# Phase two of a graph and expert kernel: gathers asked for at another distance, two flows on their own spans, degrees counted one phase sooner

## The chip, the cores and the metric

The kernel runs on one core of one Trainium2 chip. The metric is the device time of one execution in microseconds; the time before is 3418.66 us, the median of three runs (3414.97 to 3419.67). The engines named below are PE (matrix products), DVE (vector work), ACT (activations and copies), POOL (which here issues nearly only gathers and scatters) and SP (which issues the plain DMAs). Each works through its own list of instructions in order.

## The reference, cut to what matters

There are 3125 nodes with 256 features, 50000 edges sorted by destination, and four blocks, each a graph step and a feed-forward step. The change lies in the first two graph steps, which share one pass over the edges, and in the preparation of the third:

```python
# block 0: messages by relation type, summed by destination, then experts
transformed = jnp.einsum('ni,rio->rno', h, weight)
msg = transformed[rel_type, src] * norm
out = jax.ops.segment_sum(msg, dst, num_segments=h.shape[0])
...
out = out + combine[:, e:e + 1] * y      # 8 experts, the top 2 of them weighted
# block 1: messages by species and edge features
msgs = embed_table[node_z][senders] * W
agg = jax.ops.segment_sum(msgs, receivers, num_segments=node_feats.shape[0])
out = jnp.concatenate([node_feats, agg], axis=1) @ W_comb + b_comb
# block 2 and 3 need the edges of each node: attention and a maximum
m = jax.ops.segment_max(e, edge_dst, num_segments=N)
```

## The kernel before

**Edges.** The 50000 edges are padded to 392 windows of 128, in 49 groups of 8. The rows of two windows of a group are gathered by one call of `fetch_rows` (L810), which issues two indirect DMAs on POOL (L153, tile `g`); we call that a row pair. A group has four pairs. Twelve pairs have buffers (`G_PAIRS`), so pair n can only be gathered when the group of pair n - 12 has been summed. `make_hots` (L821) makes the group's 0/1 mask on DVE, and `add_up` (L829) multiplies mask and rows on PE (L834), copies the result out of PSUM on ACT (L837) and has SP store it to a table of partial sums in DRAM (L839, L842): 288 rows for each group, `part1` in phase one and `part0` in phase two.

**Phase one** (100 to 649 us) takes the pairs of block 1, from the table of species, and beside them PE makes the table of block 0 (`chunk`, L618). One background step `next(bg)` runs at every second pair; the background is `ranks` (L1180), which finds where each node's edges begin, its degree, and in which rows of the partial sums they lie. It ends at 288 us and the rest of the phase has none.

**Phase two** (`stage_two`, L908) takes the pairs of block 0 in 392 slots, eight for each group: slot 8g + j. The first twelve pairs have been asked for at the end of phase one. In every odd slot from slot 9 on one more pair is asked for; the mask of the next group is made in slot j = 1, the group is summed in slot j = 7, and `between` (L1143) then advances everything else by a slot. At slot 16 stands `all_edges` (L722), a branch that is not taken with sorted edges.

**Flows.** Node tiles of 128 are worked on in 13 flows, flow 0 of one tile and the others of two. A flow is born when all its edges have been summed (slots 32, 64, 96, ...; 32 apart). It has its partial sums gathered (`load_p`, tile `p`, one gather for each tile, waiting for the stores that it reads) 6 slots later (`LOAD_AFTER`), starts 14 slots after its birth (`START_AFTER`), and runs through three parts, each a generator that is spread evenly over a span of slots: `route` (L960, 22 steps over 24 slots: adds the sums, norm, top 2), `experts` (L1005, 32 steps over 30) and `combine` (L1033, 34 steps over 30, with the sums of phase one, and the tables of block 2). One part is never worked on by two flows. After slot 392 the flows that are left run without a clock.

**Background of phase two.** At every second slot one step runs of `by_degree` (L1273) and then `records` (L1352). `by_degree` orders the nodes by degree: it counts the nodes of each degree (L1282 compares, L1288 adds, one product with ones and a scan: `base`), then for each of 25 tiles it ranks the nodes (L1305 adds `base`, L1306 the nodes of earlier tiles, L1307 those ahead in this tile, all three into one PSUM bank; L1309 picks the rank), and then turns ranks into order (`both`, L1325: a compare at L1328 and three at L1330 for each tile, and a product at L1340). `records` then makes edge scores from 100 loads of attributes, stores them (L1384), and fetches for each of 25 tiles the window of its nodes' edges (`k_w`, a gather on POOL).

The order of instructions on each engine is that of the program: no scheduler moves them.

Of the kernel before, what the change touches and what calls it, by code (L numbers as in the profile page):

```python
# [9 lines left out]
F32 = mybir.dt.float32  # L10
# [9 lines left out]
P = 128  # L20
N = 3125
NT = 25
# [37 lines left out]
G_PAIRS, F_BUFS = 12, 4  # L60
# [14 lines left out]
LAST = [8 * g - 9 if g < NG else NW - 2 for g in DONE]  # L75
SEGS = [g - 1 if g < NG else NG for g in DONE]
assert all(2 * P * (t + k) <= n * SEG for (t, k), n in zip(FLOWS, SEGS))
LOAD_AFTER, START_AFTER = 6, 14
AB = 4


# [27 lines left out]
BG_EVERY = 2  # L109
# [3 lines left out]
def tile_gnn_ffn(ctx: ExitStack, tc: tile.TileContext, a: dict, out: bass.AP):  # L113
    nc = tc.nc
# [52 lines left out]
    ones = per.tile([P, P], F32, name="ones")  # L167
# [216 lines left out]
    wb = w1st.enter_context(tc.tile_pool(name="wb", bufs=1))  # L384
# [72 lines left out]
    with tc.If(uns > 0):  # L457

        rec = dram.tile([E, RW], F32, name="rec")
        with tc.tile_pool(name="srt", bufs=1) as ep, tc.tile_pool(name="srt2", bufs=2) as eb, \  # L460
# [12 lines left out]
            beg = before_nodes(ep, eb, hif, lof, "s_")  # L473
# [10 lines left out]
            for b in range(ET // BT):  # L484
# [11 lines left out]
                for i in range(BT):  # L496
                    j = b * BT + i
# [173 lines left out]
    def late_weights(pool, w):  # L671

        def loads(name, dst, src):
            w[name] = dst
            nc.sync.dma_start(dst, src)

        def rows(m, name):
            k, n = m.shape
            return pool.tile([P, k // P, n], F32, name="w_" + name, bufs=1), m.rearrange("(k p) n -> p k n", p=P)

        def same(src, n):
            return bass.AP(tensor=src.tensor, offset=src.offset, ap=[[0, P], [1, n]])

        loads("rw0", *rows(a["L0_ffn_router_w"], "rw0"))
        loads("b01", pool.tile([P, 16], F32, name="w_b01", bufs=1), a["L0_ffn_b1"])
        loads("b02", pool.tile([8, D], F32, name="w_b02", bufs=1), a["L0_ffn_b2"])
        yield
        w["01"], w["02"] = (wbig[:, i * 16 * D : (i + 1) * 16 * D].rearrange("p (e k f) -> p e k f", e=8, k=2) for i in range(2))
        for e in range(8):
            nc.sync.dma_start(w["01"][:, e], a["L0_ffn_w1"][e].rearrange("(k p) f -> p k f", p=P))  # L690
            nc.sync.dma_start(w["02"][:, e], a["L0_ffn_w2"][e].rearrange("(f p) d -> p f d", p=P))
            yield
        loads("c", *rows(a["L1_gnn_W_comb"], "c"))
        yield
        nc.sync.dma_start(wfa[:, :, :D], a["L2_gnn_W_func"].rearrange("(k p) n -> p k n", p=P))
        loads("bc", pool.tile([P, D], F32, name="w_bc", bufs=1), same(a["L1_gnn_b_comb"], D))
        for i in range(2):
            loads(f"aw{i}", pool.tile([P, D], F32, name=f"w_aw{i}", bufs=1), same(a["L2_gnn_W_att"][:, i * D : (i + 1) * D], D))
        loads("wr", pool.tile([P, D], F32, name="w_wr", bufs=1), same(a["L1_ffn_wr"], D))
        yield  # L700
# [76 lines left out]
    def stage_one():  # L777
# [24 lines left out]

        sh = w1st.enter_context(tc.tile_pool(name="sh", bufs=2))
        w = {}
        bg, loads = ranks(sh), late_weights(sh, w)
        pairs = NW // 2
        rows, feats, hots = {}, {}, {}
        at = {"rows": 0, "feats": 0, "chunk": LEAD}
# [35 lines left out]
        with tc.tile_pool(name="ea", bufs=1) as ea, psums(t=2, pw=3, agg=1, w=2):  # L844
# [35 lines left out]
            for k in range(pairs):  # L880
                g = k // 4
# [26 lines left out]
    def stage_two(eb, bg, w, rows, hots, fetch_rows, make_hots, add_up):  # L908
# [199 lines left out]

        class Flow:

            PARTS = ((route, 22, 24), (experts, 32, 30), (combine, 34, 30))

            def __init__(self, q):
                self.q, self.part, self.gen, self.born, self.loaded = q, 0, None, slot, False
# [1 line left out]
            def step(self, slot, older, fast):  # L1116
                if self.part == 3:
                    return
                make, total, span = self.PARTS[self.part]
                if not self.loaded and slot >= self.born + LOAD_AFTER:  # L1120
                    self.loaded = True
                    load_p(self.q, 0)
                if slot < self.born + START_AFTER:
                    return
                if self.gen is None:
                    if any(o.part <= self.part for o in older):
                        return
                    self.gen, self.since, self.done = make(self.q), slot, 0
                due = self.done + 1 if fast else -(-total * (slot - self.since + 1) // span)
                while self.done < due:  # L1130
                    self.done += 1
                    try:
                        next(self.gen)
                    except StopIteration:
                        assert abs(self.done - 1 - total) < 3 or size(self.q) == 1, (self.part, self.done - 1)
                        self.part, self.gen = self.part + 1, None
                        return
# [3 lines left out]
        slot = 0  # L1141

        def between(fast=False):  # L1143
            nonlocal slot
            for i, f in enumerate(flows):
                f.step(slot, flows[:i], fast)
            while flows and flows[0].part == 3:
                flows.pop(0)
            if slot % BG_EVERY == 0:
                next(bg, None)  # L1150
            if slot >= 60 and slot % 2:
                next(zeros_, None)
            slot += 1

        made = 0
        make_hots(0, nrmW)
        for g in range(NG):
            if g == 2:
                all_edges(bank())
            for j in range(8):  # L1160
                if j == 1:
                    make_hots(g + 1, nrmW)
                if j % 2 and g:
                    fetch_rows()
                if j == 7:
                    add_up(g, [rows.pop(pairs + 4 * g + i) for i in range(4)], part0)
                between()
            while made < len(DONE) and DONE[made] == g + 1:
                flows.append(Flow(made))
                made += 1  # L1170
# [99 lines left out]

    kept = {}

    def by_degree(sh):  # L1273

        node, deg, beg = kept["node"], kept["deg"], kept["beg"]
        key = wb.tile([P, NT], F32, name="k_key")
        nc.vector.tensor_scalar(key, deg, 127.0, -1.0, op0=OP.min, op1=OP.mult)
        nc.vector.tensor_scalar_add(key, key, 127.0)
# [1 line left out]
        def chosen(t):  # L1280
            s = sh.tile([P, P], F32, name="k_sel")
            nc.vector.tensor_scalar(s, iota_f, key[:, t : t + 1], None, op0=OP.is_equal)  # L1282
            return s
# [2 lines left out]
        nc.vector.memset(cum, 0.0)  # L1286
        for t in range(NT):
            nc.vector.tensor_add(cum, cum, chosen(t))  # L1288
            if t % 4 == 3:
                yield  # L1290
        pk = tp(P)
        nc.tensor.matmul(pk, ones, cum, start=True, stop=True)
        tot = wb.tile([P, P], F32, name="k_tot")
        base = wb.tile([P, P], F32, name="k_base")
        nc.vector.tensor_copy(tot, pk)
        nc.vector.tensor_tensor_scan(base, ones, tot, 0.0, op0=OP.mult, op1=OP.add)
        nc.vector.tensor_sub(base, base, tot)
        rank = wb.tile([P, NT], F32, name="k_rank")
        prev = wb.tile([P, P], F32, name="k_prev")
        nc.vector.memset(prev, 0.0)  # L1300
        nxt = chosen(0)
        for t in range(NT):
            sel, nxt = nxt, (chosen(t + 1) if t + 1 < NT else None)
            pk = tp(P)
            nc.tensor.matmul(pk, ones[:1, :], base[:1, :], start=True, stop=False)  # L1305
            nc.tensor.matmul(pk, ones, prev, start=False, stop=False)  # L1306
            nc.tensor.matmul(pk, upper, sel, start=False, stop=True)  # L1307
            nc.vector.tensor_add(prev, prev, sel)
            stt(sel, sel, 1.0, pk, op0=OP.mult, op1=OP.mult, accum_out=rank[:, t : t + 1])  # L1309
            yield  # L1310
# [1228 lines left out]
```

## Time and profile before

| What | Value |
| --- | --- |
| median of three runs | 3418.66 us (3414.97 to 3419.67) |
| profiled execution, its own time | 3418.41 us |
| its span | 3416.7 us |
| phase one from its first products of edges | 100 to 649 us |
| phase two, 392 slots | 649 to 1315 us |
| flows left after the last slot | 1315 to 1470 us |
| PE, DVE, POOL busy in phase two's slots (666 us) | 528.36, 471.49, 441.43 us |

A stretch row gives, for a stretch of the span, the busy time of each engine with its number of instructions, the granted TensorE clock as a share of full speed, and the DMA's share and rate. A row of the order of time gives start, length, engine, line, operation and tiles; what stands in brackets is how long the engine had been idle before it and what ended that. A gather's bar on POOL (0.95 us) is followed by 0.30 us in which the queue issues nothing else.

### The profile page before, as it was taken

Reading aid. Unit: us, or ns where it says so; the run is one execution under the profiler, and the core shown is the slowest. Engines: PE = TensorE matmul, PEld = TensorE weight load, DVE = VectorE, ACT = ScalarE, POOL = GpSimd, SP = SyncE. Lnnn points to the kernel's source line nnn. Section 1 sums busy time; section 2 is a strip of 40 time slices with the busy share of each in tenths; the row PEclk is TensorE's granted clock in tenths of the full one; section 3 lists DMA queues with packets and bytes.
Section 4 is the critical chain, followed back from the end, with each engine's and each line's share of the span. In section 5 each row is a group of like instructions: output and inputs, shape, how many; then the busy total and the mean of one; then the engine's idle time right before and its main releaser. Section 6 shows DMA issues by size and latency. Waiting matters only on the chain. (4 is left out here: it accounts for less than half of the span.)

```text
span 3416.7 us, 36379 instructions
## 1 busy us (share of the span) xinstructions
PE 2240.7 (66%) x10325; PEld 1557.2 (46%) x10325; DVE 1678.1 (49%) x6067; ACT 898.8 (26%) x2016; POOL 1999.7 (59%) x2265
## 2 busy tenths in 40 slices
PE   4689999777888779849322585877711212259993
PEld 1334444345666557637211373756511112237672
DVE  2343333557787766533365565566723333366211
ACT  1334545312233223312110131323300000024341
POOL 3677777766666671011577777764467777732433
PEclk9889999758999889959655696888755555559997
DMA  7577777857775452031243585876233333325562
GB/s 238 183 229 245 254 253 251 255 135 228 235 235 177 111 144 80 31 130 50 80 111 104 158 262 176 266 257 188 95 90 106 105 105 106 105 76 165 166 217 81
DMA packets 246803, 553.65 MB, mean 162 GB/s; under 512 B 49584, under 2 KB 131251, under 8 KB 240174
## 3 DMA queue, kind: packets, MB, share of 16 engines
q0 software_dynamic: 103296, 283.74, 27.8%
q1 hardware_dynamic: 137624, 261.43, 23.6%
q10 hardware_dynamic: 5654, 5.88, 0.6%
q8 instruction: 90, 1.47, 0.2%
q14 instruction: 139, 1.14, 0.1%
HBM read 394.00 MB, written 156.83 MB: 161 GB/s over the span
## 5 line engine op out<-in xcount | busy, mean ns | idle before, releaser
L153 POOL DMA_INDIRECT g<-tabe,e_src x392 | 371.2, 947 | 196.2 <-issue 97.2
L153 POOL DMA_INDIRECT g_rows<-tab,srcI x413 | 402.4, 974 | 126.9 <-issue 104.8
L153 POOL DMA_INDIRECT g_row<-tab,srcI x413 | 390.6, 946 | 131.6 <-issue 119.8
L153 POOL DMA_INDIRECT g<-tabt,e_code x392 | 377.9, 964 | 151.1 <-issue 79.5
L625 PE MATMUL t<-w_big,n_xt 128*128 128x512 f32 x800 | 378.7, 619 | 0.5 <-ACT n_xt L613 0.5
L2386 DVE TENSOR_TENSOR ACC<-ACC,g_row 128x256 f32<-128x256 f32 x413 | 175.8, 426 | 341.4 <-DMA g_row<-tab,srcI 341.3
L1638 PE MATMUL tp<-ident,ACC 128*128 128x128 f32 x50 | 16.6, 435 | 420.4 <-DVE ACC L2386 420.4
L871 DVE TENSOR_TENSOR mt<-pw,g 128x512 f32<-128x512 f32 x196 | 126.7, 686 | 257.0 <-ACT p_out L837 145.6
L1970 PE MATMUL mm<-ro_xt,ro_w 128*128 128x192 f32 (+3 forms) x928 | 232.2, 401 | 28.9 <-ACT ro_h L2051 21.4
L1974 PE MATMUL y<-ro_w,ro_h 128*96 128x256 f32 (+2 forms) x1040 | 243.7, 388 | 1.5 <-ACT ro_h L2051 1.5
L625 PEld LDWEIGHTS t<-w_big,n_xt 128*128 128x128 f32 x800 | 148.8, 195 | 185.7 <-issue 184.1
L1018 PE MATMUL w<-xt,w_big 128*128 128x256 f32 (+1 forms) x832 | 214.2, 399 | 0.0
L2261 DVE SCALAR_TENSOR_TENSOR ACC<-g_rows,g_e,ACC 128x256 f32<-128x256 f32 x413 | 201.2, 487 | 13.4
L1970 PEld LDWEIGHTS mm<-ro_xt,ro_w 128*128 128x128 f32 x928 | 170.2, 205 | 73.3 <-ACT ro_h L2051 27.4
L157 POOL DMA_INDIRECT xg<-XX,ro_pos x100 | 100.8, 1008 | 174.8 <-issue 72.5
L1638 PEld LDWEIGHTS tp<-ident,ACC 128*128 128x128 f32 x50 | 7.2, 203 | 428.1 <-issue 353.2
L1974 PEld LDWEIGHTS y<-ro_w,ro_h 128*96 128x96 f32 (+2 forms) x1040 | 181.7, 180 | 44.1 <-ACT ro_h L2051 1.9
L1027 PE MATMUL w<-w_big,b_h 128*128 128x256 f32 x800 | 198.9, 387 | 1.6 <-DVE n_x L1029 1.6
L628 ACT COPY n_tst<-t 128x512 f32<-128x512 f32 x200 | 117.2, 586 | 266.7 <-PE t L625 239.7
L153 POOL DMA_INDIRECT ro_g<-yg,ro_back x100 | 99.4, 994 | 137.3 <-issue 67.4
L1018 PEld LDWEIGHTS w<-xt,w_big 128*128 128x128 f32 x832 | 162.7, 209 | 27.2 <-issue 4.9
L1027 PEld LDWEIGHTS w<-w_big,b_h 128*128 128x128 f32 x800 | 154.0, 195 | 24.2 <-DVE n_x L1029 2.0
(579 smaller groups left out, 4349.8 us busy)
## 6 DMA issues: line engine op xcount, KB each, us to landing
tabt<-n_tst SPq DMA_DIRECT2D x50, 1024.0 KB
ro_w<-in_L_ffn_blocks SPq DMA_DIRECT2D x58, 514.0 KB
ro_w<-in_L_ffn_blocks SPq DMA_DIRECT2D x58, 512.0 KB
part<-p_out SPq DMA_DIRECT2D x98, 256.0 KB
xg<-zero SPq DMA_DIRECT2D x78, 200.0 KB
f<-in_attr SPq DMA_DIRECT2D x49, 256.0 KB
b_at<-in_edge_attr SPq DMA_DIRECT2D x100, 125.0 KB
tabr<-v SPq DMA_DIRECT2D x11, 770.0 KB
```

Source lines behind the costliest of these rows:

```text
L153: return nc.gpsimd.indirect_dma_start(out=dst, out_offset=None, in_=table, in_offset=bass.IndirectOffsetOnAxis(ap=idx, axis=0))
L157: return nc.gpsimd.indirect_dma_start(out=table, out_offset=bass.IndirectOffsetOnAxis(ap=idx, axis=0), in_=src, in_offset=None)
L625: nc.tensor.matmul(pt, xt_of[t][:, k, :], wrel[:, k, 2 * i : 2 * i + 2, :].rearrange("p r d -> p (r d)"), start=(k == 0), stop=(k == 1))
L628: nc.scalar.copy(stage[0][:, o : o + 2 * D], pt)
L871: nc.vector.tensor_tensor(m, biased.pop(0), rows.pop(k + b), op=OP.mult)
L1018: nc.tensor.matmul(ph, w["01"][:, e, k, i * P : (i + 1) * P], xt[:, k, : n * h], start=(k == 0), stop=(k == 1))
L1027: nc.tensor.matmul(py, last[:, k, i * h : (i + 1) * h], w["02"][:, e - 1, k, :], start=(k == 0), stop=(k == 1))
L1638: nc.tensor.transpose(pt[:, k, :m], src[:, k * P : (k + 1) * P], ident[:m, :m])
L1970: nc.tensor.matmul(ph, w[:, o : o + P], xt[:, k, :], start=(k == 0), stop=(k == 1))
L1974: nc.tensor.matmul(py, h[:, i, s], w[:, i * D : (i + 1) * D], start=(i == 0), stop=(i == self.fc - 1))
L2261: stt(u, g[:, r, :D], e[:, r0 + r : r0 + r + 1], u, op0=OP.mult, op1=OP.add)
L2386: nc.vector.tensor_tensor(u, u, rows.pop(r), op=OP.max)
```

## The change

Four things change.

1. The counting of degrees leaves `by_degree` for a new generator `degrees`, which follows `ranks` in the background of phase one, with a step every 2 tiles instead of every 4. `base` is put in row 0 of `prev`, so the product at L1305 falls away: the product with `prev` adds it.
2. The background of phase two takes one step in each of slots 0 to 29, none in slots 30 to 55, and then one in every second slot again.
3. A row pair is asked for when twice its number is less than the slot plus `ahead`: 10 up to slot 79 (before, this distance was 16), then one more for every second slot; and never past the pairs of group g + 2. Pairs of later groups are asked for at slot 8g, four at once, from slot 112 on.
4. Flows 0 and 1 have their sums gathered 2 slots after their birth and start 5 slots after it, with a route of 11 and 14 slots. The other flows are as they were: 6, 14 and 24.

By these numbers flow 0 starts at slot 37 (before, 46) and ends its combine at slot 110 (132); flow 1 starts at slot 69 (78) and ends at 145 (164); flow 2 keeps its slots.

```diff
@@ -75,7 +75,8 @@
 LAST = [8 * g - 9 if g < NG else NW - 2 for g in DONE]
 SEGS = [g - 1 if g < NG else NG for g in DONE]
 assert all(2 * P * (t + k) <= n * SEG for (t, k), n in zip(FLOWS, SEGS))
-LOAD_AFTER, START_AFTER = 6, 14
+LOAD_AFTER, START_AFTER = (2, 2, 6), (5, 5, 14)
+NEAR, QUICK = 10, 80
 AB = 4
 
 
@@ -802,7 +803,7 @@
 
         sh = w1st.enter_context(tc.tile_pool(name="sh", bufs=2))
         w = {}
-        bg, loads = ranks(sh), late_weights(sh, w)
+        bg, loads = (step for part in (ranks(sh), degrees(sh)) for step in part), late_weights(sh, w)
         pairs = NW // 2
         rows, feats, hots = {}, {}, {}
         at = {"rows": 0, "feats": 0, "chunk": LEAD}
@@ -1108,7 +1109,7 @@
 
         class Flow:
 
-            PARTS = ((route, 22, 24), (experts, 32, 30), (combine, 34, 30))
+            PARTS = ((route, 22, (11, 14, 24)), (experts, 32, (30, 30, 30)), (combine, 34, (30, 30, 30)))
 
             def __init__(self, q):
                 self.q, self.part, self.gen, self.born, self.loaded = q, 0, None, slot, False
@@ -1117,10 +1118,12 @@
                 if self.part == 3:
                     return
                 make, total, span = self.PARTS[self.part]
-                if not self.loaded and slot >= self.born + LOAD_AFTER:
+                kind = min(self.q, 2)
+                span = span[kind]
+                if not self.loaded and slot >= self.born + LOAD_AFTER[kind]:
                     self.loaded = True
                     load_p(self.q, 0)
-                if slot < self.born + START_AFTER:
+                if slot < self.born + START_AFTER[kind]:
                     return
                 if self.gen is None:
                     if any(o.part <= self.part for o in older):
@@ -1146,13 +1149,13 @@
                 f.step(slot, flows[:i], fast)
             while flows and flows[0].part == 3:
                 flows.pop(0)
-            if slot % BG_EVERY == 0:
+            if slot < 30 or slot >= 56 and slot % BG_EVERY == 0:
                 next(bg, None)
             if slot >= 60 and slot % 2:
                 next(zeros_, None)
             slot += 1
 
-        made = 0
+        made, asked = 0, G_PAIRS
         make_hots(0, nrmW)
         for g in range(NG):
             if g == 2:
@@ -1160,7 +1163,9 @@
             for j in range(8):
                 if j == 1:
                     make_hots(g + 1, nrmW)
-                if j % 2 and g:
+                ahead = NEAR if slot < QUICK else NEAR + (slot - QUICK) // 2
+                while asked < 4 * g + G_PAIRS and 2 * asked < slot + ahead:
+                    asked += 1
                     fetch_rows()
                 if j == 7:
                     add_up(g, [rows.pop(pairs + 4 * g + i) for i in range(4)], part0)
@@ -1270,9 +1275,9 @@
 
     kept = {}
 
-    def by_degree(sh):
-
-        node, deg, beg = kept["node"], kept["deg"], kept["beg"]
+    def degrees(sh):
+
+        deg = kept["deg"]
         key = wb.tile([P, NT], F32, name="k_key")
         nc.vector.tensor_scalar(key, deg, 127.0, -1.0, op0=OP.min, op1=OP.mult)
         nc.vector.tensor_scalar_add(key, key, 127.0)
@@ -1286,7 +1291,7 @@
         nc.vector.memset(cum, 0.0)
         for t in range(NT):
             nc.vector.tensor_add(cum, cum, chosen(t))
-            if t % 4 == 3:
+            if t % 2:
                 yield
         pk = tp(P)
         nc.tensor.matmul(pk, ones, cum, start=True, stop=True)
@@ -1295,15 +1300,23 @@
         nc.vector.tensor_copy(tot, pk)
         nc.vector.tensor_tensor_scan(base, ones, tot, 0.0, op0=OP.mult, op1=OP.add)
         nc.vector.tensor_sub(base, base, tot)
-        rank = wb.tile([P, NT], F32, name="k_rank")
         prev = wb.tile([P, P], F32, name="k_prev")
         nc.vector.memset(prev, 0.0)
+        nc.vector.tensor_copy(prev[:1, :], base[:1, :])
+        yield
+
+        kept.update(prev=prev, chosen=chosen)
+
+    def by_degree(sh):
+
+        node, deg, beg = kept["node"], kept["deg"], kept["beg"]
+        prev, chosen = kept["prev"], kept["chosen"]
+        rank = wb.tile([P, NT], F32, name="k_rank")
         nxt = chosen(0)
         for t in range(NT):
             sel, nxt = nxt, (chosen(t + 1) if t + 1 < NT else None)
             pk = tp(P)
-            nc.tensor.matmul(pk, ones[:1, :], base[:1, :], start=True, stop=False)
-            nc.tensor.matmul(pk, ones, prev, start=False, stop=False)
+            nc.tensor.matmul(pk, ones, prev, start=True, stop=False)
             nc.tensor.matmul(pk, upper, sel, start=False, stop=True)
             nc.vector.tensor_add(prev, prev, sel)
             stt(sel, sel, 1.0, pk, op0=OP.mult, op1=OP.mult, accum_out=rank[:, t : t + 1])
```

## The prediction

> **What bounds the kernel now.** I read the page's first two parts first. No engine is full over the span, so I went on to the busy times of stretches, one for each stage that the change touches (columns: stretch, its length, busy time and instructions of each engine, granted TensorE clock, share and rate of DMA).
>
> ```profile
> 288.00:356.00 68.00, 68.00 (x326) 31.73 (x326) 22.73 (x44) 34.22 (x66) 48.62 (x52) 1.00 0.77 251
> 642.00:714.00 72.00, 48.23 (x254) 28.74 (x252) 38.15 (x144) 5.28 (x9) 51.96 (x55) 0.64 0.63 184
> 741.00:763.00 22.00, 15.24 (x43) 10.53 (x43) 19.91 (x96) 1.75 (x4) 15.11 (x16) 0.50 0.62 186
> 797.00:864.00 67.00, 47.89 (x251) 34.51 (x243) 45.41 (x169) 16.15 (x39) 40.60 (x42) 0.81 0.69 221
> 864.00:918.00 54.00, 46.96 (x251) 35.27 (x254) 43.30 (x164) 17.71 (x40) 36.50 (x38) 0.91 0.73 235
> ```
>
> The first row is phase one where the moved degree steps will lie: PE is full, DVE a third busy. The second is the opening of phase two: POOL shows 52 of 72 us, but each gather holds the queue longer than its bar, as the next view shows. In the third DVE is full. The last two reach from group 11 to group 20; the fifth is 32 slots of the steady state, with PE 47 and DVE 43 of 54 us. Then the order of time on POOL, and the instructions that wait for it:
>
> ```profile
> 642.72 0.94 POOL L153 DMA_INDIRECT g<-tabt,e_code  x1 [0.30 <-issue]
> ...
> 680.62 0.94 POOL L153 DMA_INDIRECT g<-tabt,e_code  x1 [0.30 <-PE w L1305]
> 681.87 0.95 POOL L153 DMA_INDIRECT g<-tabt,e_code  x1 [0.30 <-issue]
> 686.64 0.95 POOL L153 DMA_INDIRECT g<-tabt,e_code  x1 [3.82 <-PE w L1305]
> ...
> 714.23 0.94 POOL L153 DMA_INDIRECT p<-part,p_row  x1 [0.30 <-issue]
> 719.74 0.48 DVE L967 SCALAR_TENSOR_TENSOR n_x<-p,p_m,n_x 128x256 f32<-128x256 f32 x1 [14.00 <-DMA p<-part,p_row]
> ...
> 755.98 0.95 POOL L153 DMA_INDIRECT p<-part,p_row  x1 [0.30 <-issue]
> 757.23 0.95 POOL L153 DMA_INDIRECT p<-part,p_row  x1 [0.30 <-issue]
> 758.49 0.95 POOL L153 DMA_INDIRECT g<-tabt,e_code  x1 [0.31 <-PE w L1340]
> ```
>
> Fifty-four gathers lie between 642.72 and 714.23: 1.253 us each, less one gap of 3.82 us, the branch of `all_edges`. POOL runs without a pause to 760; it sets the pace of the first seven groups. The sums of flow 0 (`p`) stand behind those 54, and DVE waits 14.00 us for them: they land 5.5 us after their issue. What PE made of it, from the sums of groups 3, 8, 11 and 20:
>
> ```profile
> 687.93 1.07 PE L834 MATMUL agg<-g,s 128*32 128x256 f32 x16
> ...
> 763.07 1.94 PE L834 MATMUL agg<-g,s 128*32 128x256 f32 x16
> ...
> 796.79 1.51 PE L834 MATMUL agg<-g,s 128*32 128x256 f32 x12
> ...
> 917.93 1.94 PE L834 MATMUL agg<-g,s 128*32 128x256 f32 x16
> ```
>
> Group 7 starts at 738.30 and group 8 only at 763.07, although its rows were asked for by 737: DVE, full with the 25 `both` steps of L1328 and L1330 (0.88 us each), holds PE in between. So the opening has two bounds, POOL to slot 64 and then DVE.
>
> **The change, part by part.** I follow one clock, the start of a group's sum, against the profiled execution (span 3416.7, time 3418.41 us, 0.25 under the median of the runs).
>
> *Degrees in phase one.* 25 compares (L1282, 0.33) and 25 adds (L1288, 0.29) leave slots 0 to 12: 15.5 us of DVE, with one fp32 product (0.8), one scan and three small steps. Ranks end at 288, so the 13 steps fall from there to about 356, where DVE is free 45 of 68 us and PE is full. What covers them is PE's own load; without it they would cost their 15.5. PE gains one product: +1 us. Bounds: 0 and +15.5; near 0, since the row has the cover.
>
> *Opening, slots 0 to 31.* A rank step was L1305, L1306, L1307 at 1.87 us a step. L1305 goes, since `base` now lies in row 0 of `prev`. What remains is a ring: L1306 starts, 0.83 later DVE adds to `prev` (0.29), 0.06 later the next L1306. That is 1.2 us (0.92 at best, DVE's own issue between 686 and 688). One step a slot now: 25 in slots 0 to 24, 20 `both` in 26 to 29. Group 0 ends at 662.7 as before, since ACT waits for a store there, and seven steps hide ahead of it. Then: 18 x 1.2 = 21.6, two sums at 1.94, the branch 1.1, the tail of the ranks with one mask and one `both` 3.1, 20 x 0.88 = 17.6, a last product 0.7. Group 3 starts at 710.7 and ends at 712.6, not 689.0. Lateness here: +23.
>
> *The sums of flow 0, two slots behind.* POOL now meets them behind 44 gathers, at 642.7 + 44 x 1.253 + 3.8 = 701.6. They need group 3's store: copy 0.6 and two issues at 0.5 put it at 713.8. Stores of this tile took from issue to the end of ACT's wait 6.6 us (first row here to the last, as ACT shows it) and 10.5 at worst:
>
> ```profile
> 659.82 0.33 SPq L842 DMA_DIRECT2D part<-p_out  x1
> 660.11 0.59 ACT L837 COPY p_out<-agg 128x512 f32<-128x512 f32 x1 [10.83 <-DMA part<-p_out]
> ...
> 666.48 0.59 ACT L837 COPY p_out<-agg 128x512 f32<-128x512 f32 x1 [5.79 <-DMA part<-p_out]
> ```
>
> I take 6.6, the last before the opening, where the weight loads had ended: 720. So POOL, in order, stands still for 18 us, and everything behind it with it: the gathers of groups 5 and on, whose buffers would be free. This is the wait that the change adds. Bounds: 4 us (steps at 0.92, store as quick as the 5.5 of the sums) and 22. Flow 0's rows land at 725.5; its route is a chain of some 15 us on one tile, alone on DVE now, and ends near 740.
>
> The Trainium skill's page "DMA: Bandwidth & Descriptors", section "Rules for kernel authors", says to issue a DMA early and wait for it late; asking two slots behind the store speaks against that. Its section on the anatomy of one DMA gives about 2 us of fixed cost, most of it the receipt of the write; the store here took 6.6. With 2 the stop would be 14 us and the whole sum some 4 us lower, by estimate.
>
> *Slots 32 to 95.* POOL: 721.3 + 14 pairs x 2.506 + one load of 1.25 = 757.7 for the last row of group 8, whose sum starts near 760 instead of 763.07. `both` no longer stands in the way; POOL does. The sums of flow 1 are asked for at slot 66, behind two pairs of group 9: 762.7, second tile 763.9, landed 769.4. DVE comes to slot 69 near 756 and waits 13 us: the 14.00 us of before returns at flow 1. Its two-tile route needs some 10 us of DVE, 9 of hops to PE and ACT and 5 of records between them: 793 at slot 83. From there the kernel of before has a like stretch, experts and combine without a route, from 796.79 to 818.97 in 16 slots, 1.39 a slot. Twelve slots at 1.3 (POOL's floor is 1.25): group 11 at 808, where it was 796.79. Lateness +11; but combine 0 is half done and experts 1 a third, work that before had yet to come.
>
> *Slots 96 to 167.* Here that work is missing: of a full flow, 0.48 of its experts, 0.27 of its combine and a quarter of its route in 71 slots, so 0.22, 0.12 and 0.11 per 32 slots. An experts part is 64 products of 0.41 and 64 of 0.38 on PE, 32.6 us, and 16 x 0.48 on DVE; of the others I put 10 on PE and 14 on DVE each, an estimate from their rows. PE was busy 94.9 and DVE 88.7 of 121 us, 43 and 40 per 32 slots; they fall to some 34 and 36. POOL keeps 16 x 2.506 + 4 x 1.25 = 45.1, the floor. The steady pace was 53.7 (864.21 to 917.93). I take 47, near the floor because the other loads fall well under it. 808 + 71/32 x 47 = 912.3 for group 20, against 917.93: -5.6. Bounds: 45.1 gives -10, 53.7 gives +9.
>
> *After that.* Flow slots are as before. From slot 112 the four pairs of a group are asked for at once. They waited for one sum anyway; the sums at the group's slot 6 stand one pair (2.5 us) later, inside a stop for their store (6.58 us at 864.99): 0, bounds 0 and +8. The records end 16 slots sooner: two groups run at 11.6 us (1243.50 to 1313.34 is six) instead of 13.4: -3.6, bounds -4 and 0. Their loads on SP move past 16 slots of stores with them: 0, bounds -4 and +4 by the one stop (4.32 us at 809.67) that such a load ended on POOL. The branch stands behind 26 gathers on POOL, not 32, and costs its 3.82 as before.
>
> Sum: +1 - 5.6 - 3.6 = -8.2; 3418.4 - 8.2 = 3410.
>
> The clock is part of this. Between 655 and 683 rank steps followed one another on PE and the granted clock was 0.50. "TensorE: Matmul & The Clock Gate", Part 1, says that about 3.4 us of sustained work brings the full clock; by it the 18 steps would take some 5 us less and the forecast would be 3406 by estimate. The row, not the rule, stands in my sum.
>
> **Rivals.**
>
> *The held POOL is never made good (slower).* Place: slots 34 and 69. If slots 96 to 167 run at 53.7 per 32 as before, group 20 starts at 927 and the time is +1 + 9.3 - 3.6 = +6.7: 3425. It decides above 50.7 us per 32 slots, where the sum is nil. For it: 797 to 918 went at 54.6 per 32 slots with less combine than the steady state has, so chains between engines count there, not sums. Against: PE loses a fifth of its load.
>
> *POOL is hardly held (faster still).* Steps at 0.92 and a quick store bring the sums at 712; group 11 at 800, group 20 at 904: -13.6, in all -16: 3402. For it: 0.96 of the clock between 683 and 689. Against: 0.50 before and after.
>
> *It is hidden or given back in the windows.* From slot 270 `k_w` gathers stand behind four pairs at once, up to three more than before (7.5 us), and DVE already waits 21.2 us for them in 9 waits. 1.5 us in each of some six groups is +9: 3419, no change.
>
> **How the numbers follow.** A measurement of this kernel can tell 0.2%, 6.8 us. Forecast 0.36 (3402 to 3414; under 3411.8 in nearly all), quick opening 0.13, given back 0.20, never made good 0.26, and 0.05 for phase one paying all its 15.5. Faster: 0.49; same 0.20; slower 0.31. The likeliest is 3410. The range takes the quick opening with the floor pace (3394) and the slow rival with some loss in phase one (3430).
>
> **What would show it.** Right: no L1288 rows after 649; 25 `both` gone from 741 to 763; a gap of 10 to 20 us on POOL ahead of the first `p`, ended by the store; a DVE wait of about 13 us at L967 for flow 1; group 8 near 760, group 11 near 808, group 20 near 912. Wrong: group 3 before 700, POOL without a gap, or a pace near 54 to slot 167; longer `k_w` waits; PE gaps between 288 and 356.

## The result and the profile after

The changed kernel takes 3436.06 us (median of six, 3431.95 to 3439.11) where the kernel before takes 3419.16 on the same chip (median of six): the ratio is 1.0049, 95% interval 1.0036 to 1.0062. It is 17 us slower; 3410 was forecast. Its profiled execution took 3431.95 us with a span of 3430.2, so the profiles show 13.5 us of the difference.

The stretches of the changed kernel that answer to those shown of before, with the row of before for slots 96 to 167 in the fence after it (stretch, length, busy time and instructions of PE, weight loads, DVE, ACT and POOL, granted clock, DMA share and rate):

```profile
288.00:356.00 68.00, 68.00 (x314) 31.74 (x314) 36.25 (x93) 34.16 (x66) 48.49 (x52) 1.00 0.75 248
642.00:714.00 72.00, 46.80 (x246) 30.95 (x248) 47.28 (x212) 3.52 (x6) 41.36 (x44) 0.67 0.52 156
806.00:931.00 125.00, 85.85 (x437) 61.08 (x440) 81.20 (x290) 29.40 (x65) 84.09 (x87) 0.81 0.73 234
931.00:985.00 54.00, 47.33 (x250) 36.07 (x246) 43.19 (x164) 17.76 (x41) 36.25 (x38) 0.91 0.75 235
```

```profile
797.00:918.00 121.00, 94.85 (x501) 69.78 (x497) 88.72 (x332) 33.86 (x79) 77.10 (x80) 0.85 0.71 227
```

The degrees lie in phase one (DVE 36.25 us where it was 22.73) and PE is as full as before: they are hidden. The steady state from 931 on is the old one. Between group 11 (806) and group 20 (931) PE has 9 us and DVE 7.5 us less to do than before had in the same 72 slots, and yet they take 125 us in place of 121.

The order of time of the changed kernel (start, length, engine, line, what; in brackets the idle time before it and what ended that):

```profile
660.39 0.79 PE L1319 MATMUL w<-k_prev,ones 128*128 128x128 f32 x2 [10.58 <-ACT p_out L838]
712.33 1.08 PE L835 MATMUL agg<-g,s 128*32 128x256 f32 x8
722.63 0.94 POOL L154 DMA_INDIRECT p<-part,p_row  x1 [19.23 <-issue]
726.09 0.48 DVE L968 SCALAR_TENSOR_TENSOR n_x<-p,p_m,n_x 128x256 f32<-128x256 f32 x1 [12.62 <-DMA p<-part,p_row]
764.05 1.06 PE L835 MATMUL agg<-g,s 128*32 128x256 f32 x14
773.08 0.48 DVE L968 SCALAR_TENSOR_TENSOR n_x<-p,p_m,n_x 128x256 f32<-128x256 f32 x1 [9.30 <-DMA p<-part,p_row]
779.86 0.69 PE L935 MATMUL w<-ident,ag 128*128 128x128 f32 x2 [12.79 <-DVE ag L1043]
805.97 1.07 PE L835 MATMUL agg<-g,s 128*32 128x256 f32 x16
849.50 0.47 PE L935 MATMUL w<-ident,ag 128*128 128x128 f32 x1 [14.46 <-DVE ag L1043]
930.65 1.94 PE L835 MATMUL agg<-g,s 128*32 128x256 f32 x16
```

The four `agg` rows are groups 3, 8, 11 and 20 (line 835, which was 834; the sums of a flow are used in line 968, which was 967; the rank products are lines 1319 and 1320). POOL stops for 19 us ahead of the sums of flow 0, as foreseen (the row says "issue", so the profile itself names no releaser), and group 8 is only 1.0 us late after it. Next DVE stands 9.30 us for the sums of flow 1, and queued behind that wait on DVE is the first step of flow 0's combine (`ag`), for which PE stands 12.79 us; group 11 is 9.2 us late. At 849.50 PE stands for `ag` again, one flow on, but not behind a sum: the 9.30 us are DVE's only wait for sums from 764 to 931. There DVE waits for the attribute rows of the records (`b_at`) and does the first steps of flow 2 ahead of `ag`.

How late a group starts against the kernel before (us, one profiled execution each) shows where each run of the study lost or won its time; "end" is the span. The start of the kernel before is in the second column.

| group | before | changed | b_degrees | b_fetch_2 | b_flows | a_flows | a_pout_2 | a_deep | a_zeros | b_best |
| --- | --- | --- | --- | --- | --- | --- | --- | --- | --- | --- |
| 3 | 687.9 | +24.4 | -3.8 | -2.9 | -2.5 | +26.3 | +16.2 | +25.2 | +25.4 | -2.9 |
| 5 | 707.2 | +29.5 | -2.2 | +1.3 | +21.6 | +10.4 | +20.9 | +30.2 | +30.7 | -1.8 |
| 8 | 763.1 | +1.0 | -2.6 | -8.5 | +14.0 | -5.3 | -6.1 | +2.3 | -0.1 | -2.8 |
| 11 | 796.8 | +9.2 | +5.3 | -2.2 | +21.7 | +3.2 | +6.0 | +13.0 | +9.1 | -2.5 |
| 20 | 917.9 | +12.7 | +3.5 | -0.7 | +22.5 | +6.1 | +6.4 | +6.5 | +3.7 | -4.4 |
| 28 | 1025.8 | +13.0 | +3.6 | -1.0 | +24.2 | +6.6 | +7.1 | +10.0 | +5.5 | -3.9 |
| 42 | 1243.5 | +13.0 | +1.9 | -2.0 | +18.6 | +8.7 | +8.4 | +7.9 | +6.5 | -10.0 |
| 48 | 1313.3 | +11.2 | +2.0 | -2.2 | +16.9 | +8.4 | +8.2 | +6.1 | +6.3 | -10.2 |
| end | 3416.7 | +13.5 | -0.9 | +1.5 | +26.1 | +8.0 | +7.7 | +8.2 | +6.6 | -10.2 |

What stands at group 11 is, within 8 us, what stands at the end. Between groups 8 and 11 the changed kernel loses 8.2 us, but b_degrees, b_fetch_2 and a_flows, which have the old flows, lose 6 to 9 us there too, and b_degrees is as fast as the kernel before: this loss by itself does not speak against the early flows. A single profile may lie several us from its kernel's median (b_flows 6 above, a_deep 5 below), so times are compared by the ratios to the kernel before on the same chip:

| run | what differs | us | ratio to before, 95% interval |
| --- | --- | --- | --- |
| changed | the whole change | 3436.06 | 1.0049 (1.0036 to 1.0062) |
| b_degrees | degrees alone | 3420.03 | 1.0004 (0.9995 to 1.0012) |
| b_fetch_2 | degrees, gathers | 3417.72 | 0.9992 (0.9983 to 1.0001) |
| b_flows | degrees, early flows | 3438.71 | 1.0058 (1.0044 to 1.0072) |
| a_flows | without the early flows | 3430.60 | 1.0030 (1.0019 to 1.0041) |
| a_cadence | without the new cadence | 3439.73 | 1.0061 (1.0047 to 1.0075) |
| a_fetch | without the new gather rule | 3433.01 | 1.0036 (1.0022 to 1.0050) |
| a_flow0, a_flow1 | flow 0, flow 1 old | 3434.59, 3434.03 | 1.0044 (1.0030 to 1.0057), 1.0041 (1.0027 to 1.0054) |
| a_deep | changed, b_at loads 6 ahead | 3432.00 | 1.0037 (1.0023 to 1.0050) |
| a_zeros | changed, zero stores from slot 168 | 3429.95 | 1.0028 (1.0019 to 1.0037) |
| a_pout_2 | changed, 4 p_out buffers | 3426.40 | 1.0022 (1.0013 to 1.0031) |
| b_best | degrees, 4 p_out buffers, zero stores from slot 168 | 3413.14 | 0.9985 (0.9975 to 0.9994) |

Six runs (a_pout, b_fetch, b_cadence, b_zeros, a_all, b_best2) fell on two other chips, on which the kernel before takes 4072 and 4070 us; they are compared with that alone and told of by themselves.

### The profile page after: what moved, and what is told of

It is laid out like the page before. It is cut to its first block, busy times and chain, and to the rows that moved or that the text cites. A ratio compares the mean times of both kernels' runs of the same rounds, so it can differ in the third digit from the quotient of the medians.

```text
span 3430.2 us, 36283 instructions
## 1 busy us (share of the span) xinstructions
PE 2226.1 (65%) x10275; PEld 1548.7 (45%) x10275; DVE 1681.3 (49%) x6068; ACT 899.3 (26%) x2016; POOL 1996.2 (58%) x2265
## 5 line engine op out<-in xcount | busy, mean ns | idle before, releaser
L154 POOL DMA_INDIRECT g_row<-tab,srcI x413 | 391.1, 947 | 131.5 <-issue 119.3
L1983 PEld LDWEIGHTS mm<-ro_xt,ro_w 128*128 128x128 f32 x928 | 169.7, 205 | 67.4 <-ACT ro_h L2064 21.6
```

Source lines behind the costliest of these rows:

```text
L154: return nc.gpsimd.indirect_dma_start(out=dst, out_offset=None, in_=table, in_offset=bass.IndirectOffsetOnAxis(ap=idx, axis=0))
L1983: nc.tensor.matmul(ph, w[:, o : o + P], xt[:, k, :], start=(k == 0), stop=(k == 1))
```

## The experiments

**Each part left out.** My theory after the two traces was that the crowded opening is the cause: rank and `both` steps in slots 0 to 29 hold group 3, and the records then start 16 slots sooner. Three runs leave one part of the change out each, one leaves out all but the degrees.

```
a_flows    -LOAD_AFTER, START_AFTER = (2, 2, 6), (5, 5, 14)
           +LOAD_AFTER, START_AFTER = (6, 6, 6), (14, 14, 14)
           -(route, 22, (11, 14, 24))
           +(route, 22, (24, 24, 24))
a_cadence  -if slot < 30 or slot >= 56 and slot % BG_EVERY == 0:
           +if slot % BG_EVERY == 0:
a_fetch    -ahead = NEAR if slot < QUICK else NEAR + (slot - QUICK) // 2
           -while asked < 4 * g + G_PAIRS and 2 * asked < slot + ahead:
           -    asked += 1
           +if j % 2 and g:
                fetch_rows()
b_degrees  all three edits at once
```

> The changed kernel with the old numbers for flows 0 and 1 (sums asked for 6 slots behind their store, routes of 24 slots, started 14 slots behind). My theory (the rank and both steps crowd into slots 0 to 29, hold group 3 by 24 us, and the records then start 16 slots sooner beside the zero stores on SP): the stop of 19 us on POOL ahead of the first p goes, but group 3 is as late as in the changed kernel (about 712) and the waits for b_at stay near 30 us: 3428 to 3436. Rival A (the sums asked for too early are what costs, by the stop on POOL): 3416 to 3422, like before. Rival B (gather distance 10 and bursts of four): 3434 to 3439, no difference.

> The changed kernel with the background on its old cadence (one step every second slot, no pause). My theory: group 3 starts within 5 us of the kernel before (688 to 693), the sums of flow 0 find their store landed or nearly so, the records start some 8 slots later, the b_at waits fall to 20 us or less: 3414 to 3422. Rival A (early sums): the stop on POOL for the store stays, 3430 to 3438. Rival B (gathers): 3432 to 3439.

> The changed kernel with the old rule of the row gathers (one pair in each odd slot from group 1 on). My theory: the distance costs little, group 3 is still at 712, the windows at group 40 are not late by 26 us any more, which was recovered anyway: 3431 to 3438. Rival A: no difference. Rival B (the distance of 10 slots and the bursts of four cost the 17 us): 3416 to 3424.

> The kernel before with the degrees counted in phase one and nothing else of the change: flows, gathers and cadence are the old ones, the rank step has two kinds of product in place of three. My theory: phase one loses 0 to 1 us, the 25 both steps leave the stretch 741 to 763 in part because the rank steps start 14 slots sooner, one at every second slot; group 8 a few us sooner: 3410 to 3419. Rival A and rival B: the same 3410 to 3419, since their parts are not in it. A rival C (the degree steps cost their 15.5 us in phase one): 3430 to 3436.

Measured: 3430.60, 3439.73, 3433.01 and 3420.03. My theory fell with a_cadence, which has group 3 on time (-2.4) and was expected at 3414 to 3422: it is as slow as the changed kernel, and 22 us late from group 11 on. a_fetch cannot be told from the changed kernel by its interval, and its profile is 17 us late at groups 11 and 20. In a_flows the lateness falls from +26.3 at group 3 to -5.3 at group 8, although POOL stops there for nearly as long:

```profile
724.83 0.94 POOL L154 DMA_INDIRECT p<-part,p_row  x1 [15.22 <-issue]
```

So neither a late group 3 nor a stop of 15 us on POOL costs up to group 8. b_degrees cannot be told from before: the moved degrees and the product taken out of the rank step, taken together, neither cost nor win anything that shows.

**One flow left early.** The same numbers for one flow alone:

```
a_flow1  LOAD_AFTER, START_AFTER = (2, 6, 6), (5, 14, 14)   route (11, 24, 24)
a_flow0  LOAD_AFTER, START_AFTER = (6, 2, 6), (14, 5, 14)   route (24, 14, 24)
```

> The changed kernel with flow 1 alone on its old numbers (sums 6 slots behind, start 14 slots behind, route of 24 slots); flow 0 stays early. Theory F with the loss at flow 1 (DVE stands 9 us for its sums and its route lies in the way of the experts of flow 0): group 8 stays near +1, groups 10 to 13 start within 5 us of before, 3428 to 3432 like the run with both flows old. If flow 0 is the cause (the stop of 19 us on POOL): group 10 stays at +10 or more, 3434 to 3438. Theory W: 3432 to 3437.

> The changed kernel with flow 0 alone on its old numbers; flow 1 stays early. If flow 1 is the cause: 3433 to 3438. If flow 0 is (its sums hold POOL, its route and experts lie in the opening): 3428 to 3432. If only both together cost: 3429 to 3432 in this run and in the one with flow 1 old.

Measured: 3434.03 and 3434.59, neither told apart from the changed kernel nor from each other. Either of them brings group 11 down (+1.8 and +7.3) and is at +10.7 and +11.7 by group 20. By its range each run alone would have blamed the other flow, so neither can be singled out. Their intervals also overlap that of a_flows (1.0019 to 1.0041): how much of the loss one early flow makes is not shown.

**The loads of the records and the zero stores.** Between 764 and 931 DVE waits 31 us for `b_at`. Two runs take that wait away by different means: loads further ahead, or no zero stores beside them on SP.

```
a_deep   ats[b] = sh.tile([EP, AB, 64], F32, name="b_at", bufs=7)    (4)
         for b in range(0, 6 * AB, AB):                                (3 * AB)
             part(b + 6 * AB)                                          (3 * AB)
a_zeros  if slot >= 168 and slot % 2: next(zeros_, None)               (60)
```

> The changed kernel with the attribute loads of the records (b_at) six steps ahead in place of three, in seven buffers in place of four. Theory W (the 31 us in which DVE waits for b_at between 764 and 931 keep the pace of slots 96 to 167 at 56 us per 32 slots): these waits fall under 15 us, group 20 starts some 5 to 12 us sooner, 3424 to 3431. Theory F (the early flows hold POOL and DVE up to group 10, and afterwards the chains of flows 0 and 1 between PE, ACT and DVE set the pace): the waits fall and other waits take their place, 3433 to 3438.

> The changed kernel with the zero stores (xg<-zero, 84 of 200 KB on SP) begun in slot 168 in place of 60. Theory W: the loads of b_at no longer stand behind them, the waits fall under 15 us, 3422 to 3430, unless the later slots pay. Theory F: the group starts up to group 10 stay as late as they are (+9 to +14), 3432 to 3438.

Measured: 3432.00 and 3429.95. The waits of DVE from 764 to 931 (us in total, times, longest) in the changed kernel, in a_deep and in a_zeros, a fence each:

```profile
DVE b_at L1390 <- DMA b_at<-in_edge_attr: 30.9, 17, 4.9
DVE n_x L968 <- DMA p<-part,p_row: 9.3, 1, 9.3
```

```profile
DVE n_x L968 <- DMA p<-part,p_row: 16.7, 4, 9.5
DVE b_at L1390 <- DMA b_at<-in_edge_attr: 6.9, 4, 3.6
```

```profile
DVE n_x L968 <- DMA p<-part,p_row: 15.9, 3, 11.1
DVE b_at L1390 <- DMA b_at<-in_edge_attr: 14.6, 8, 5.5
```

Of the wait for `b_at` 24 and 16 us are gone, and 7 us of them come back as waits for sums. From group 11 to group 20 the runs take 114.6 and 115.7 us, the changed kernel 124.7: the loads were worth 9 to 10 us in this stretch. Less of it stays: a_deep had lost 4 us more by group 11, and at group 28 the two runs are 3.0 and 7.5 us ahead of the changed kernel. PE still stands for `ag` in a_deep, at the same step:

```profile
846.05 0.48 PE L935 MATMUL w<-ident,ag 128*128 128x128 f32 x1 [12.71 <-DVE ag L1043]
```

Each theory of these runs was half right: the waits for `b_at` did hold the stretch, and other waits took part of their place. a_zeros wins by its ratio (0.28% over before, not 0.49%, though the intervals just touch); for a_deep the median is 4 us better, within the interval.

**One part alone, and the wait ahead of group 0.** In the changed kernel PE's first rank product waits 10.58 us for ACT's last copy of phase one, which waits for a `p_out` buffer whose store stands behind weight loads on SP. A fourth buffer takes that wait away. Beside it, two parts of the change alone on top of b_degrees, and the old order of work with the zero stores moved.

```
a_pout, a_pout_2    o = sh.tile([P, 2 * D], F32, name="p_out", bufs=4)   (3)
b_fetch, b_fetch_2  b_degrees with the new gather rule
b_cadence           b_degrees with the new cadence
b_zeros             kernel before, zero stores from slot 168
b_flows             b_degrees with the new numbers for flows 0 and 1
b_best              b_degrees, p_out bufs=4, zero stores from slot 168
```

> The changed kernel with four p_out buffers in place of three, so that ACT's last copy of phase one need not wait for a store behind the weight loads. If my sum was right but for the seven rank steps that did not hide ahead of group 0: PE's wait of 10.6 us ahead of its first rank product goes, group 3 starts at 700 to 705 in place of 712, the stop of POOL ahead of the first p falls from 19 to some 8 to 12 us, and group 10 is 6 us sooner or more: 3426 to 3431. If the loss comes only at flow 1 and from the loads of the records: group 3 is sooner, but group 13 is as late as before, 3433 to 3438.

> The kernel before with the degrees in phase one and the new rule of the row gathers, nothing else. From the three runs that each left one part out (3431, 3440, 3433 against 3420 with none) the parts would add up to: flows +11, gathers +9, cadence +2. If they add up: 3426 to 3432, with POOL's gathers of later groups ahead of the sums and the windows. If the gathers cost only beside the early flows: 3418 to 3422.

> The kernel before with the degrees in phase one and the new cadence of the background (every slot to 30, a pause to 56), nothing else. If the parts add up: 3419 to 3424. If the crowded opening (group 3 at 712) costs by itself, since the work that it holds up is not made good: 3427 to 3434.

> The kernel before with the zero stores begun in slot 168 in place of 60. If the records' loads and the stores of the sums standing beside the zero stores cost the old kernel time too (17.5 us of b_at waits on DVE between 764 and 931): 3410 to 3416. If only the changed kernel, whose records start 16 slots sooner, pays for it: 3417 to 3421.

On the chip where the kernel before takes 4072.17 us these gave 1.0067 (1.0045 to 1.0089), 1.0045 (1.0029 to 1.0062), 1.0018 (0.9994 to 1.0042) and 0.9991 (0.9972 to 1.0010). The expected times, all made for a kernel of 3419 us, can't be compared. Two of the kernels, and the missing third part, were run again on a chip of the first kind:

> The kernel before with the degrees in phase one and the early flows 0 and 1, nothing else. If the early flows are the main loss (the parts add up to flows +11, gathers +9, cadence +2): 3428 to 3434, group 10 late by 8 us or more. If they cost only with the long gather distance or the crowded opening: 3418 to 3423.

> The kernel before with the degrees in phase one and the new rule of the row gathers alone, on a chip of the speed of the first runs if it falls on one. If the parts add up: 3426 to 3432. If the gathers cost only beside the early flows: 3418 to 3422.

> The changed kernel with four p_out buffers. If the rank steps that did not hide ahead of group 0 are what made it slower: group 3 some 8 us sooner and 3426 to 3431. If not: group 3 sooner, group 13 as late as in the changed kernel, 3433 to 3438.

> The kernel before with the degrees in phase one, four p_out buffers and the zero stores begun in slot 168; flows, gathers and cadence old. If the zero stores cost the old order too, as they cost the changed kernel 6 us, and PE's 9.5 us ahead of group 0 are worth part of themselves: 3406 to 3414. If POOL sets the opening and the loads of the records are hidden there: 3416 to 3421.

Measured: 3438.71, 3417.72, 3426.40 and 3413.14. On top of the degrees, the early flows alone make as much loss as the whole change (more than was expected of them); the gathers alone make none. How, the order of time of b_flows shows:

```profile
711.32 0.95 POOL L154 DMA_INDIRECT p<-part,p_row  x1 [0.30 <-issue]
714.77 0.48 DVE L968 SCALAR_TENSOR_TENSOR n_x<-p,p_m,n_x 128x256 f32<-128x256 f32 x1 [22.96 <-DMA p<-part,p_row]
718.05 0.79 PE L1317 MATMUL w<-k_prev,ones 128*128 128x128 f32 x2 [17.07 <-DVE k_prev L1319]
728.77 1.94 PE L835 MATMUL agg<-g,s 128*32 128x256 f32 x16
```

POOL is not held at all here (0.30 us). The sums of flow 0 are asked for 3 us sooner than in the kernel before (714.23) and land 5 us sooner, but DVE now comes to the step that uses them nine slots earlier and stands there for 22.96 us, where it stood for 14.00. Behind it on DVE are rank steps, PE waits 17.07 us for the first of them (10.00 in the kernel before), and group 5 (last row) is 21.6 us late, as group 11 still is. At flow 1, where the kernel before has no such wait, it repeats: 9.42 us on DVE, 14.46 on PE. The length of the first wait is not the measure, though: in a_cadence, which has the same early flows and old cadence, it is 15.20 us, and group 5 is 21.9 us late all the same. What the two runs share is the place of the wait, nine slots sooner in the order of DVE.

In a_pout_2 PE's first rank product starts at 650.99 after 0.73 us of idle time, group 3 at 704.14, and POOL's stop is less than half:

```profile
650.99 0.49 PE L1319 MATMUL w<-k_prev,ones 128*128 128x128 f32 x2 [0.73 <-ACT p_out L838]
704.14 2.36 PE L835 MATMUL agg<-g,s 128*32 128x256 f32 x20
714.31 0.94 POOL L154 DMA_INDIRECT p<-part,p_row  x1 [8.68 <-issue]
```

The kernel takes 0.27% less than the changed one, by the ratios, some 9 us, as the first of its two expectations had it. b_best is 0.15% faster than the kernel before (0.06 to 0.25): the only run whose interval lies under that kernel, by less than the 0.2% I set myself as the bound.

**Both causes taken away at once.**

```
a_all    changed kernel: p_out bufs=4, zero stores from slot 168, b_at bufs=5 and 4 ahead
b_best2  the same three on b_fetch
```

> The changed kernel with four p_out buffers, the zero stores from slot 168 and the b_at loads four steps ahead in five buffers. If the two failed steps are the whole miss: 3436 - 10 (buffer) - 6 (zero stores) and some more from the deeper loads, 3412 to 3420, and group 20 no later than the kernel before. If the early flows cost by themselves: group 11 stays at +5 or more to the end, 3420 to 3427.

> The degrees in phase one and the new rule of the gathers with the same three covers, old flows and old cadence. If the covers are worth the same here: 3404 to 3412, and some 12 us under the changed kernel with its covers, the price of early flows and crowded opening. If POOL and the windows set the time: 3412 to 3418.

Both fell on a second chip of the slow kind (before 4070.40): 1.0074 (1.0045 to 1.0103) and 1.0063 (1.0043 to 1.0083). There the two can't be told apart, and both are slower than before. So the question of this pair, whether the two failed steps are the whole miss, is not answered for the first kind of chip, and on the second kind the covers didn't save the change.

What these chips do differently shows only in part. The busy times of the engines over the span, of b_zeros there and of the kernel before as profiled at first:

```profile
PE 2359.2 (58%) x10325; PEld 1603.4 (40%) x10325; DVE 1676.5 (41%) x6067; ACT 890.8 (22%) x2016; POOL 2000.2 (49%) x2265
```

```profile
PE 2240.7 (66%) x10325; PEld 1557.2 (46%) x10325; DVE 1678.1 (49%) x6067; ACT 898.8 (26%) x2016; POOL 1999.7 (59%) x2265
```

DVE, ACT and POOL have the same busy time and PE 5% more, so most of the 632 us between the two spans are waits (b_zeros differs from the kernel before in the zero stores alone). There the degrees and the gather rule together cost 0.45%, where they cost nothing on the others (b_fetch and b_fetch_2 are one kernel). Why was not followed up.

## Why the prediction was wrong

Against the profiled execution I had 8.2 us less; 13.5 more came out, a miss of 21.7. By my own clock, the start of a group:

- **Phase one** (+1, bounds 0 and +15.5): right. PE full in both, DVE up by 13.5 us, b_degrees at 1.0004, and phase two's first gather at 641.6 (642.7 before).
- **"Seven rank steps hide ahead of group 0"**: failed. The first rank product starts at 660.39, not ahead of ACT's late copy but behind it, so none hid and group 0 began 8.6 us late. The error was covered by another of the opposite sign: I held all steps at the half clock of before, and from group 0's end (671.3) to group 3 (712.3) they took 41 us where I had 48. Group 3 came at 712.3, for a forecast of 710.7, from two wrong terms. That the wait is worth about 9 us to the end, a_pout_2 shows.
- **The stop of POOL** (18 us, 701.6 to 720): right, 19.23 us to 722.63, which is 6.5 us after SP had issued group 3's store (6.6 forecast; the 2 us that I set beside it stand on the Trainium skill's page for DMAs that GpSimd issues, and this store goes by SP). That it matters was not: a_flows has 15.22 us of it and group 8 early, b_flows has none and group 5 late by 21.6. The gathers are far enough ahead to bear it.
- **Slots 32 to 95**: right. Group 8 at 764 for 760, DVE's wait at flow 1 9.3 us for 13, group 11 at 806.0 for 808, lateness +9.2 for +11. What I didn't name is what stands behind this wait, flow 0's `ag`, for which PE stands 12.79 us.
- **Slots 96 to 167, pace 47 us per 32 slots**: the step that failed. They took 124.7 us, 55.4 per 32 slots, where 104.3 was forecast: 20.4 of the 21.7 us. Of these 1.5 us are a slip: group 11 is summed in slot 95 and group 20 in slot 167, 72 slots, where I counted 71 (so the old pace there was 53.8, not 54.6). The load of DVE fell as I said, to 36.1 per 32 slots (36 forecast), that of PE to 38.2 only (34 forecast). The time did not follow. Over this stretch the kernels need 121.1 (before), 119.3 (b_degrees), 122.7 (b_fetch_2), 122.0 (b_flows), 124.0 (a_flows) and 121.5 us (a_pout_2), whatever the early flows had already done. I had put the pace between POOL's floor and the old pace by the sum of busy times, and engines that are 65 to 70% busy and wait for one another are not set by that sum.
- What set it instead is shown for 9 to 10 us within the stretch: the waits for `b_at`, mostly gone in a_deep (114.6) and halved in a_zeros (115.7), of which 3.0 and 7.5 us are still won at group 28. Such a wait need not bound the stretch: b_degrees has 29.7 us of it and takes 119.3. For the other 9 us I can only argue; their cause stays open. PE's row at 849.50 is one case: with flow 1's experts done early, PE had nothing queued but `ag`, which stood on DVE behind waits for `b_at` and the first steps of flow 2. This stretch of the changed kernel has PE busy 6.43 of 25 us:

```profile
829.00:854.00 25.00, 6.43 (x38) 3.60 (x34) 16.53 (x60) 2.63 (x6) 16.39 (x17) 0.66 0.72 233
```

- **After that** (-3.6 for the end of the records): -1.5 from group 20 to the last group, and +2.3 after the slots. Of the rival "given back" nothing shows: DVE's waits for `k_w` are no longer than before (20.7 us, 9 waits, where it was 21.2 in 9). The lateness of +26.4 at group 40, +13.0 at group 42, is there in b_degrees too (+15.7 and +2.0), which gathers by the old rule.
- **The rivals.** The one on the slower side came true as to its place in time and its sign: the pace of 55.4 lies above its point of 50.7 (50.0 by the right count). Its price (+6.7) was too low, since I took the old pace as the worst, and its cause was misnamed: a_flows makes POOL's stop good by group 8. What b_flows never makes good is the time DVE and PE stand behind a sum that has not landed; in the changed kernel the early flows cost some 6 us in the profiles, all of it before group 8 (against a_flows 6.3 us there, 6.0 at group 11, 5.5 at the end).
- **The Trainium skill's page** "DMA: Bandwidth & Descriptors", section "Rules for kernel authors" (issue early, wait late), was set beside this change only for POOL's 18 us. b_flows shows it on DVE: issued 3 us sooner and waited for nine slots sooner, the wait grew from 14.00 to 22.96 us.
- **The clock** ("between 655 and 683 rank steps followed one another"): a misreading. In the kernel before PE stood idle until 660.75 and the rank steps start at 668.00; they ran at 0.50 to 683. In the changed kernel 1.2 us a step held to 672 only; at the full clock behind that a step took 0.92 us.

The parts do not add up. By the medians the early flows cost 19 us alone (b_flows over b_degrees) and 5.5 with the rest of the change around them (changed over a_flows, intervals that overlap). The dense cadence costs 13 us without the early flows (a_flows over b_fetch_2, which differ in it alone; the intervals lie apart) and nothing that shows with them (changed over a_cadence). The traces agree with one reading, which is not shown: the dense cadence brings the rank steps out from behind DVE's wait, but pays for PE's wait ahead of group 0 itself. A run of the cadence alone on the first kind of chip, and one with early sums but a late start of the routes, would test it and were not made.

## What to carry to other kernels

To ask for data sooner helps only as far as it lands sooner; the instruction that uses it should not move up further than that, for its wait becomes the wait of everything queued behind it (17.07 us on PE in b_flows). Moving work ahead of a stretch need not make the stretch shorter when no engine in it is full, as slots 96 to 167 showed: look first at which wait ends last there, and take that one away by itself before counting on the sum of busy times. Before packing work into an idle span, look at what ends that span, since the packed work may need the same event.

## What the runs showed of the hardware

Neither the idle span ahead of it nor a fixed time of work tells the granted clock in these rows. Rows of the changed kernel after PE's 10.58 us of idle time, with the rank steps one behind another:

```profile
664.00:668.00 4.00, 3.92 (x15) 2.95 (x13) 3.00 (x13) 0.00 (x0) 2.97 (x4) 0.50 0.53 178
668.00:672.00 4.00, 3.98 (x24) 2.28 (x24) 1.70 (x8) 0.49 (x1) 3.09 (x4) 0.50 0.53 172
676.00:680.00 4.00, 3.33 (x28) 2.46 (x32) 3.34 (x18) 0.00 (x0) 0.00 (x0) 1.00 0.21 73
```

The granted clock stayed at 0.50 from 660 to 672, some 12 us in which PE was busy for 11, and was 1.00 from 676 to 692. The Trainium skill's page "TensorE: Matmul & The Clock Gate", Part 1, gives about 3.4 us of sustained work for this; here it took more than three times as long, and the measurement decides. In a_pout_2, where PE had been idle for 0.73 us only, the first of the same products ran at 0.49 us in place of 0.79. But from 655 to 659, with PE busy all the time, the clock was at 0.50 there too, and at 1.00 again from 661:

```profile
655.00:659.00 4.00, 4.00 (x16) 3.17 (x14) 3.19 (x14) 0.00 (x0) 3.07 (x4) 0.50 0.96 274
661.00:669.00 8.00, 5.87 (x40) 4.33 (x44) 6.47 (x32) 0.59 (x1) 6.17 (x7) 1.00 0.62 194
```

And one kernel, the same instructions and bytes, took 3419 us on some chips and 4072 on others of the same type, on which the worth of a part of the change also differed (degrees with gathers: 0.9992 and 1.0045).
